# Attention stage: the next mask's fetch put one step ahead of its conversion, and the grid's ReLU and normalization put later in ScalarE's order

## The chip, the cores and the metric

The kernel runs on one core of one Trainium2 chip. The time is that of one execution on the device in microseconds (us), the median of several runs: three here, 2698.76 to 2705.61 us, median 2701.66 us. A core has five engines with an instruction stream each: TensorE (PE in the profile; PEld are its weight loads), VectorE (DVE), ScalarE (ACT), GpSimd (POOL) and SyncE (SP, which only issues transfers here). Each executes its own stream strictly in its order; a semaphore holds an instruction until what it needs is there, and all that stands behind it on the same engine waits with it.

## The reference, cut to what matters

Four layers follow one another on eight batches of 512 x 512 values. The change lies where the first two overlap.

```python
# layer 0, the "grid": finite differences, then a ReLU
df = -gradv_Af + gradvv_Bf * 0.5
x = jnp.maximum(f + df * dt[:, None, None], 0.0)
# layer 1, attention with 16 heads of 32
x = _ln(src) * (1.0 + scale) + shift
scores = einsum('bhqd,bhkd->bhqk', q / sqrt(32), k) + attention_bias
scores = where(src_mask, -inf, scores)
probs = softmax(scores)
...
x = x + (ctx @ Wo + bo)
```

After it come the rest of layer 1 and two layers more (gelu feed-forward by expert, a gated low-rank response). The mask is one byte per score, 512 x 512 for a batch, the same for all heads.

## The kernel before, in words

`attention_stage` works in *units*. A unit is one batch `b`, one group `c` of four heads and one quarter `r` of the query rows: 16 units make a batch, and I number them as *steps* t = 4c + r, 0 to 15. The order of the work is written out by hand in the loop at L1137: nearly every instruction is pinned to program order on its engine (`pin`), so a line's place in the loop is its place in the engine's stream.

In iteration i of the loop three units are under way. `scores` (L1003) has put four heads' scores into four PSUM banks `s0` to `s3` at the end of the iteration before. `softmax(now, u)` for u = 0 and 1 (L1015) takes two heads each: VectorE forms bias minus scores with its minimum (L1022, `bt<-s,bt`, `mn`), which frees the scores' bank, and ScalarE takes the exponential (L1027). `turned(old, u)` (L1033) transposes the probabilities of the unit before on TensorE into one of two PSUM buffers of the tag `tr`, and VectorE or ScalarE copies them out (`pt`, L1052 and L1054); TensorE cannot transpose into a buffer before its last copy is done. `values` (L1056) multiplies probabilities by v, in odd steps. `add_mask` (L994) lets GpSimd add the mask to the bias of the next unit, and `load_bias` (L982) has SP fetch the bias of three units on.

Between these stand two kinds of extra work:

- `fill(b, t)` (L927) yields a batch's projections and what prepares the next batch n = b + 1. In step 9, inside `k_block`, `x1_in(n, c)` (L601) transposes the next batch's normalized input four times (`xtr`) into the same two `tr` buffers; VectorE (L614) and ScalarE (L612) read them in turn. In steps 11 to 14 `x1_back` (L617) turns it back, and in steps 12 to 15 `load_mask(n, t - 12)` first issues the transfer of a quarter of the next batch's mask (`mask_in`, `mu`, 64 KB, on SP) and at once its conversion to bf16 times -1e30 on ScalarE (`mask_out`, `mk`, L593).
- `grid_step` (L854) runs layer 0 for the next batches in small operations on VectorE, listed in `GRID` (L830) by a phase j. Seen from a batch's own steps, phase 8 of the next batch lies at the end of step 0, phase 14 at the end of step 6, 15 and 16 at the end of steps 7 and 8. `x0` and `x1` (phases 8 and 14) finish two of four row slices; ScalarE then applies the ReLU (L804) and issues a transfer of one edge row into that slice (L806, `x<-xed`, 2 KB). `s1` (phase 15) takes the statistics of the slice on VectorE (L812), which need the ReLU and, for the second half, the edge row. `n0` and `n1` (phases 15 and 16) form a shift on VectorE (L819, `gsh`), and ScalarE normalizes two rows (L823).

`grid_gate(i)` (L741) is a one-column addition on GpSimd at the start of an iteration. It reads the last result of VectorE's grid work, so that GpSimd's additions (L998) start only after it. In iteration 7 of a batch the result that it reads is the slice that the ReLU has just been given.

The program gives each transfer of SP and ACT one of eight completion counters in turn, and an issue first waits for the previous transfer with its counter.

Of the kernel before, what the change touches and what calls it, by code (L numbers as in the profile page):

```python
# [15 lines left out]
AF = mybir.ActivationFunctionType  # L16
# [4 lines left out]
NB = 8  # L21
S = 512
D = 512
P = 128
R = 4
# [519 lines left out]
def attention_stage(  # L545
# [12 lines left out]
    nc = tc.nc  # L558
    with ExitStack() as ctx:
# [4 lines left out]
        pin = tc.keep_in_program_order  # L564
# [21 lines left out]
        def mask_in(b, r):  # L586
            mu = pp.tile([P, S], U8, name=f"mu_{b}_{r}", tag="mu", bufs=2)
            pin(nc.sync.dma_start(mu, a["mask"][b, 0].rearrange("(p r) k -> r p k", r=R)[r]))
            mask[b, r] = mu
# [3 lines left out]
            pin(nc.scalar.activation(m, mask[b, r], AF.Copy, scale=NEG))  # L593
            mask[b, r] = m

        def load_mask(b, r):
            mask_in(b, r)
            mask_out(b, r)


        def x1_in(b, c):  # L601
            tag, bufs = ("tr", 2) if b or c < 2 else (f"s{c}", 1)
# [87 lines left out]

        gs = {}
        L, M = slice(0, D - 1), slice(1, D)

        def gv(out, x, y, op):
# [72 lines left out]
        def grid_op(n, op):  # L769
            key, p = op[0], int(op[1])  # L770
            f = gs[n, "f"]
            rows = slice(2 * p, 2 * p + 2)
            e = xt[n][:, rows, :] if p < 2 else None
            if key == "q":
                t = gs[n, "q", p]
                gv(t, t, f[:, rows, :], ALU.mult)
            elif key in "egcab":
                o = 2 * p + dict(e=0, g=2).get(key, 1)
                t = gs[n, key, p]
                gv(t, t, f[:, o : o + 2, :], ALU.mult)  # L780
            elif key == "w":
                t = gs[n, "q", p]
                gv(t, gs[n, "q", p + 1], t, ALU.subtract)
            elif key in "CG":
                gv(e, e, gs.pop((n, key.lower(), p)), ALU.add)
            elif key == "+":
                gv(e[:, :, L], e[:, :, L], gs[n, "q", p][:, :, M], ALU.add)
            elif key == "-":
                gv(e[:, :, M], e[:, :, M], gs.pop((n, "q", p))[:, :, L], ALU.subtract)
            elif key == "A":  # L790
                gv(e[:, :, M], e[:, :, M], gs.pop((n, "a", p))[:, :, L], ALU.add)
            elif key == "B":
                gv(e[:, :, L], e[:, :, L], gs.pop((n, "b", p))[:, :, M], ALU.add)
            elif key == "x":
                ends = e[:, :, 0 : D : D - 1]
                gv(ends, ends, gs[n, "ghost"][:, rows, :], ALU.add)
                pin(
                    nc.vector.scalar_tensor_tensor(
                        e, e, grid["dth"][:, n : n + 1], f[:, 2 * p + 1 : 2 * p + 3, :],
                        ALU.mult, ALU.add,  # L800
                    )
                )
                gs["last"] = e[:, 0, 0:1]
                pin(nc.scalar.activation(e, e, AF.Relu))  # L804
                x, k = ((xt[n][0:1, 0, :], n), (xt[n][P - 1 : P, R - 1, :], NB + n))[p]
                pin(nc.scalar.dma_start(x, grid["xed"][k : k + 1, :]))  # L806
            elif key == "s":
                st = small.tile([P, 2, 6], F32, name=f"gst_{n}_{p}", tag="gst", bufs=2)
                mv = small.tile([P, 2, 2], F32, name=f"gmv_{n}_{p}", tag="gmv", bufs=2)
                rs = small.tile([P, 2], F32, name=f"grs_{n}_{p}", tag="grs", bufs=2)  # L810
                for r in range(2):
                    pin(nc.vector.bn_stats(st[:, r, :], e[:, r, :]))  # L812
                    pin(nc.vector.bn_aggr(mv[:, r, :], st[:, r, :]))
                gs[n, "st"] = mv, rs
            elif key == "n":
                mv, rs = gs[n, "st"]
                sh = small.tile([P, 2], F32, name=f"gsh_{n}_{p}", tag="gsh", bufs=2)
                pin(
                    nc.vector.scalar_tensor_tensor(sh, mv[:, :, 0], -1.0, rs, ALU.mult, ALU.mult)  # L819
                )  # L820
                for r in range(2):
                    pin(
                        nc.scalar.activation(  # L823
                            e[:, r, :], e[:, r, :], AF.Identity, bias=sh[:, r : r + 1],
                            scale=rs[:, r : r + 1],
                        )
                    )


        GRID = {  # L830
# [96 lines left out]
        def fill(b, t):  # L927

            n = b + 1
            jobs = []  # L930
            if b == 0:
                if t == 0:
                    homes = (("m", 1), ("tr", 2), ("tr", 2), ("ctx", 1))
                    for m in range(4):
                        jobs.append(v_block(0, m, *homes[m]))
                        jobs.append(grid_early(j) for j in (m + 3,))
                    jobs.append(grid_early(7) for _ in range(1))
                    jobs.append(mask_out(0, r) for r in (2, 3))
                elif t == 1:
                    jobs.append(add_bv() for _ in range(1))  # L940
                elif t in (2, 3, 4, 7):
                    jobs.append(x1_back(0, (2, 3, 4, 7).index(t)) for _ in range(1))
            if n == NB:
                if t == 0:
                    head["fill"] = halves(b)
                jobs.append(
                    next(head["fill"], None)
                    for _ in range({0: 2, 7: 2, 8: 2, 11: 2, 12: 2, 13: 0, 14: 2, 15: 0}.get(t, 1))
                )
            elif t in (0, 4, 8):  # L950
                jobs.append(q_block(b, t // 4 + 1))
            elif t in (1, 5, 9):
                turn = (lambda c: x1_in(n, c)) if t == 9 else None
                jobs.append(k_block(b, t // 4 + 1, turn=turn))
            elif t in (2, 3, 6, 7):
                if b:
                    jobs.append(o_block(b - 1, (2, 3, 6, 7).index(t)))
            elif t == 11:
                jobs.append(q_block(n, 0))
            elif t == 13:  # L960
                jobs.append(k_block(n, 0))
            else:
                jobs.append(v_block(n, (10, 12, 14, 15).index(t)))
            if n < NB:
                if t in (11, 12, 13, 14):
                    jobs.append(x1_back(n, t - 11) for _ in range(1))
                if t >= 12:
                    jobs.append(load_mask(n, t - 12) for _ in range(1))
            elif t == 8:
                jobs.append(head_stats() for _ in range(1))  # L970
            elif t in (10, 11):
                jobs.append(head_norm(r) for r in (2 * t - 20, 2 * t - 19))
            elif t in (13, 15):
                jobs.append(head_turn(c) for c in (t - 13, t - 12))
            for j in jobs:
                yield from j
# [135 lines left out]
        n = len(units)  # L1112
# [24 lines left out]
        for i in range(n + 2):  # L1137
            now = units[i] if i < n else None
            old = units[i - 1] if 1 <= i <= n else None
            two = units[i - 2] if i >= 2 else None  # L1140
            jobs = fill(now[0], 4 * now[1] + now[2]) if now else iter(())
            grid_gate(i)
            if i + 1 < n:
                add_mask(*units[i + 1])
            grid_step(i - 1, grid_pow)
            pair = two and two[2] % 2 == 1
            if pair:
                values(two[0], two[1], two[2] // 2)
            for u in range(2):
                if old:  # L1150
                    turned(*old, u)
                if now:
                    softmax(*now, u)
                next(jobs, None)
            if old and old[2] == R - 1:
                inverse(*old[:2])
            drain(jobs)
            split = pair and two[2] == R - 1
            if split:
                grid_step(i, lambda n, j: grid_sums(n, j, late=False))  # L1160
                divide(two[0], two[1])
            if i + 3 < n:
                load_bias(*units[i + 3])
            if now and now[0] and now[1:] == ((2, 1) if now[0] < NB - 1 else (3, 3)):
                nc.sync.dma_start(x1d[now[0] - 1], xt[now[0] - 1])
            if now and now[0] == NB - 1:
                head_load(4 * now[1] + now[2])
            grid_step(i, lambda n, j: grid_sums(n, j, early=not split))
            grid_step(i, grid_loads)
            if i + 1 < n:  # L1170
                scores(*units[i + 1])
# [893 lines left out]
```

## Time and profile before

| what | us |
|---|---|
| median of three runs | 2701.66 |
| the profiled execution | 2701.51 |
| its span, first to last instruction | 2699.7 |
| TensorE busy in it | 2649.8 |
| VectorE, GpSimd, ScalarE busy | 1930.8, 1480.9, 960.9 |
| attention: first scores to last | 70.8 to 1077 |
| feed-forward and the rest | 1106 to 2699 |

The profile comes from one execution. Its page has busy times, the chain of work that ended last, and groups of instructions with the idle time before them and what ended it. The chain of waits lists, per engine, who waited for whom: total us, times, longest. The timeline lists instructions by start and duration, with the idle time before one in square brackets and who ended it. Step lengths below are read off the timeline as the distance between the first scores matmuls (`s<-kt,qt`) of two units that follow each other. From 1106 us to the end TensorE works without a gap in stretches of 48.35 us, which the change doesn't touch.

### The profile page before, as it was taken

The page shows a single profiled execution, that of the slowest core. Times are in us where ns is not written, and L with a number is a line of the kernel's source. Part 1 is how long each engine was busy: PE and PEld are TensorE (multiplying, and loading weights), DVE is VectorE, ACT ScalarE, POOL GpSimd, SP SyncE. Part 2 cuts the span into 40 slices and gives each one's busy share as a digit, 9 for nine tenths or more (in the row PEclk, how much of TensorE's full clock was granted, in tenths as well). Part 3 has the DMA queues.
Part 4 walks back from the last instruction along what each step waited for, and adds up shares of the span by engine and source line. Part 5 has one row for each costly group of instructions (what it writes and reads, how often), then busy time and mean ns, then how long its engine had stood idle before and what let it go on. Part 6 is the DMA issues. An engine that isn't in the chain of part 4 may idle for free.

```text
span 2699.7 us, 39350 instructions
## 1 busy us (share of the span) xinstructions
PE 2649.8 (98%) x14182; PEld 1959.2 (73%) x14182; DVE 1930.8 (72%) x3538; ACT 960.9 (36%) x1997; POOL 1480.9 (55%) x1090
## 2 busy tenths in 40 slices
PE   7999999999999999999999999999999999999998
PEld 4455555555555555788888888888888888888887
DVE  7888898989898756576666656656555766666665
ACT  2566666666666666212212211210111211211221
POOL 3455565655555655366566465555555555555543
PEclk9999999999999999999999999999999999999999
DMA  8765757666676554644453543455335346345421
GB/s 308 253 217 194 247 193 242 212 215 231 230 240 211 167 170 157 194 144 117 138 156 98 162 146 100 148 156 154 120 116 184 127 150 194 124 145 198 121 100 42
DMA packets 241760, 460.31 MB, mean 171 GB/s; under 512 B 33848, under 2 KB 77440, under 8 KB 232478
## 3 DMA queue, kind: packets, MB, share of 16 engines
q1 hardware_dynamic: 237754, 447.04, 49.2%
q0 software_dynamic: 3360, 10.68, 3.0%
q8 instruction: 113, 1.85, 0.3%
q14 instruction: 81, 0.66, 0.1%
q10 hardware_dynamic: 452, 0.07, 0.0%
HBM read 398.43 MB, written 55.09 MB: 168 GB/s over the span
## 4 chain that ended last, share of the span: by engine, by line
PE 90%; DVE 4%; DMA 3%; ACT 1%; SPq 1%; issue 1%; POOL 0%; ACTq 0%; DVEq 0%; POOLq 0%
PE u L1208 29%; PE y L1208 28%; PE tr L570 8%; PE s L567 5%; PE o L567 4%; PE ctx L567 4%; PE pq L567 4%; PE pv L567 3%; PE pk L567 3%; DMA mu<-in_mask 2%; DVE bt L1022 1%; PE l L251 1%; DMA rd<-rt 1%; DVE x L697 1%; DVE pt L1052 1%
## 5 line engine op out<-in xcount | busy, mean ns | idle before, releaser
L998 POOL TENSOR_TENSOR bt<-bt,mk 128x1024 f32<-128x1024 f32 x256 | 543.7, 2148 | 72.6 <-DMA bt<-in_bias 67.2
L1208 PE MATMUL y<-wo,act 128*128 128x256 f32 x2560 | 566.3, 380 | 0.0
L1208 PEld LDWEIGHTS y<-wo,act 128*128 128x128 f32 x2560 | 484.5, 190 | 71.6 <-issue 6.7
L1027 ACT ACTIVATE bt<-bt,mn 128x512 f32<-128x512 f32 x512 | 365.7, 716 | 87.7 <-DVE mn L1022 86.4
L570 PEld LDWEIGHTS tr<-ident,bt 128*128 128x128 f32 x2048 | 229.4, 142 | 159.9 <-issue 97.5
L1022 DVE CUSTOM_DVE_ANT_0 bt<-s,bt 128x512 f32<-128x512 f32 x512 | 330.8, 684 | 2.2 <-PE s L567 2.0
L1208 PE MATMUL u<-bt,wi 128*128 128x256 f32 x1440 | 330.5, 379 | 0.0
L1214 DVE TENSOR_TENSOR act<-u,u 128x512 f32<-128x512 f32 x256 | 173.2, 684 | 200.6 <-PE u L1208 132.5
L1208 PEld LDWEIGHTS u<-bt,wi 128*128 128x128 f32 x1440 | 273.5, 190 | 37.2
L570 PE MATMUL tr<-ident,bt 128*128 128x128 f32 x2048 | 278.2, 278 | 15.1 <-ACT pt L1054 12.9
L1208 PE MATMUL u<-tb,ws 128*128 128x256 f32 x1024 | 242.2, 379 | 0.0
L1054 ACT COPY pt<-tr 128x512 f32<-128x512 f32 x306 | 172.6, 581 | 179.0 <-PE tr L570 176.3
L1208 PE MATMUL y<-t,s 128*128 128x256 f32 x1024 | 227.8, 380 | 0.0
L1217 POOL TENSOR_TENSOR t<-wo,t 128x512 f32<-128x512 f32 x64 | 107.3, 1699 | 203.1 <-PE y L1208 203.1
L1052 DVE COPY pt<-tr 128x512 f32<-128x512 f32 x206 | 141.9, 689 | 106.2 <-PE tr L570 100.2
L1208 PEld LDWEIGHTS u<-tb,ws 128*128 128x128 f32 x1024 | 194.3, 190 | 26.6 <-DVE tb L1214 0.2
L1208 PEld LDWEIGHTS y<-t,s 128*128 128x128 f32 x1024 | 194.0, 190 | 26.1
L1572 ACT ACTIVATE act<-act,b 128x512 f32<-128x512 f32 x128 | 82.9, 712 | 292.8 <-DVE act L1214 292.8
L1572 ACT ACTIVATE act<-act,bi 128x512 f32<-128x512 f32 x128 | 83.8, 712 | 282.6 <-DVE act L1214 282.6
L567 PE MATMUL s<-kt,qt 32*128 32x512 f32 x1024 | 175.9, 640 | 2.0 <-DVE mn L1022 1.0
L1591 ACT COPY u<-u 128x512 f32<-128x512 f32 x64 | 36.4, 568 | 393.3 <-PE u L1208 278.2
L1214 DVE TENSOR_TENSOR x<-y,x 128x512 f32<-128x512 f32 (+1 forms) x97 | 64.7, 680 | 154.0 <-PE y L1208 103.7
(323 smaller groups left out, 4144.5 us busy)
## 6 DMA issues: line engine op xcount, KB each, us to landing
bt<-in_bias SPq DMA_DIRECT2D x256, 512.0 KB
wo<-in_W SPq DMA_DIRECT2D x32, 1024.0 KB
wi<-in_Wi SPq DMA_DIRECT2D x32, 1024.0 KB
wo<-in_Wo_e SPq DMA_DIRECT2D x32, 1024.0 KB
wi<-in_W SPq DMA_DIRECT2D x28, 1024.0 KB
td<-tt SPq DMA_DIRECT2D x22, 1024.0 KB
bt<-td SPq DMA_DIRECT2D x176, 128.0 KB
gq<-coef_q SPq DMA_DIRECT2D x21, 512.0 KB
```

What stands on the lines that cost most here:

```text
L567: pin(nc.tensor.matmul(out, lhsT=lhsT, rhs=rhs, start=start, stop=stop))
L570: pin(nc.tensor.transpose(out, src, ident))
L998: nc.gpsimd.tensor_tensor(bt, bt, mask[b, r][:, None, :].to_broadcast([P, 2, S]), ALU.add)
L1022: nc.vector.tensor_tensor_reduce(bt[:, i, :], ss[h], bt[:, i, :], -1.0, 3.0e38, ALU.add, ALU.min, mn)
L1027: nc.scalar.activation(bt[:, i, :], bt[:, i, :], AF.Exp, bias=mn, scale=-1.0, accum_out=sums[b, c][:, h, r : r + 1],)
L1052: pin(nc.vector.tensor_copy(pt[:, :, r % 2, :], tr))
L1054: pin(nc.scalar.copy(pt[:, :, r % 2, :], tr))
L1208: pin(nc.tensor.matmul(out, lhsT=lhsT, rhs=rhs, start=start, stop=stop))
L1214: pin(nc.vector.tensor_tensor(out, x, y, op))
L1217: pin(nc.gpsimd.tensor_tensor(out, x, y, op))
L1572: nc.scalar.activation(acts[g][:, k, :], acts[g][:, k, :], func, bias=bi[:, j : j + 1])
L1591: pin(nc.scalar.copy(u1, p[0]))
```

## The change

Three things move; no instruction is added or taken away, and the order on TensorE, VectorE and GpSimd stays what it was.

- `load_mask` is split. The transfer of quarter r of the next mask is issued in step 11 + r, and its conversion stays in step 12 + r. On SP each of the 28 transfers moves up by one step, past that step's two bias transfers and what lies between.
- The ReLU with its edge row transfer goes from the end of steps 0 and 6 into the next step, behind the exponentials of the first two heads (u = 0). On ScalarE it moves past one or two copies `pt` and two exponentials.
- The normalization goes in the same way from the end of steps 7 and 8 into steps 8 and 9.

With the ReLU behind it in program order, the gate of iteration 7 now waits for VectorE's result and not for the ReLU, and the ReLU waits for the gate to have read it. The transfers' counters shift too: SP's second `gq` load behind the `gf` loads in step 7 shared a counter with the edge row and now shares one with a `gf` load.

```diff
-        def load_mask(b, r):
-            mask_in(b, r)
-            mask_out(b, r)
...
-        gs = {}
+        gs, later = {}, []
...
                 gs["last"] = e[:, 0, 0:1]
-                pin(nc.scalar.activation(e, e, AF.Relu))
-                x, k = ((xt[n][0:1, 0, :], n), (xt[n][P - 1 : P, R - 1, :], NB + n))[p]
-                pin(nc.scalar.dma_start(x, grid["xed"][k : k + 1, :]))
+
+                def relu():
+                    pin(nc.scalar.activation(e, e, AF.Relu))
+                    x, k = ((xt[n][0:1, 0, :], n), (xt[n][P - 1 : P, R - 1, :], NB + n))[p]
+                    pin(nc.scalar.dma_start(x, grid["xed"][k : k + 1, :]))
+
+                later.append(relu)
...
-                for r in range(2):
-                    pin(
-                        nc.scalar.activation(
-                            e[:, r, :], e[:, r, :], AF.Identity, bias=sh[:, r : r + 1],
-                            scale=rs[:, r : r + 1],
+
+                def norm():
+                    for r in range(2):
+                        pin(
+                            nc.scalar.activation(
+                                e[:, r, :], e[:, r, :], AF.Identity, bias=sh[:, r : r + 1],
+                                scale=rs[:, r : r + 1],
+                            )
                         )
-                    )
+
+                later.append(norm)
...
                 if t >= 12:
-                    jobs.append(load_mask(n, t - 12) for _ in range(1))
+                    jobs.append(mask_out(n, t - 12) for _ in range(1))
+                if 11 <= t < 15:
+                    jobs.append(mask_in(n, t - 11) for _ in range(1))
...
                 if now:
                     softmax(*now, u)
+                while u == 0 and later:
+                    later.pop(0)()
                 next(jobs, None)
```

## The prediction

> **What bounds the kernel now.** First the page: who owns the chain that ended last.
>
> ```profile
> span 2699.7 us, 39350 instructions
> ...
> PE 2649.8 (98%) x14182; PEld 1959.2 (73%) x14182; DVE 1930.8 (72%) x3538; ACT 960.9 (36%) x1997; POOL 1480.9 (55%) x1090
> ...
> PE 90%; DVE 4%; DMA 3%; ACT 1%; SPq 1%; issue 1%; POOL 0%; ACTq 0%; DVEq 0%; POOLq 0%
> ```
>
> TensorE is the bound, so a change elsewhere counts only where it makes TensorE wait. Next the chain of waits:
>
> ```profile
> ACT mk L593 <- DMA mu<-in_mask: 56.7, 14, 6.3
> ...
> POOL gate L746 <- ACT x L804: 26.4, 7, 3.8
> ...
> PE tr L570 <- ACT pt L1054: 12.9, 14, 2.1
> ```
>
> ScalarE stands 56.7 us in front of the mask's conversion, and TensorE 12.9 us in front of ScalarE's copies. The timeline of batch 3 joins the two (steps 13 and 14):
>
> ```profile
> 567.28 1.14 PE L567 MATMUL s<-kt,qt 32*128 32x512 f32 x8
> ...
> 573.18 0.63 ACT L593 ACTIVATE mk<-mu 128x512 bf16<-128x512 uint8 x1 [5.09 <-DMA mu<-in_mask]
> ...
> 574.34 0.66 PE L570 MATMUL tr<-ident,bt 128*128 128x128 f32 x4 [0.87 <-ACT pt L1054]
> ...
> 577.11 1.14 PE L567 MATMUL s<-kt,qt 32*128 32x512 f32 x8
> ...
> 581.00 0.63 ACT L593 ACTIVATE mk<-mu 128x512 bf16<-128x512 uint8 x1 [2.84 <-DMA mu<-in_mask]
> ...
> 582.16 0.66 PE L570 MATMUL tr<-ident,bt 128*128 128x128 f32 x4 [0.73 <-ACT pt L1054]
> ...
> 584.93 1.14 PE L567 MATMUL s<-kt,qt 32*128 32x512 f32 x8
> ```
>
> Mask late, copy late, transpose late: the steps take 9.83 and 7.82 us. With no wait on TensorE they take 8.73 (step 11 of batch 6, same work) and 6.87 (step 14 of batches 1 and 6). Last, steps 8 and 9, where the normalization goes:
>
> ```profile
> 524.28 8.43 POOL L998 TENSOR_TENSOR bt<-bt,mk 128x1024 f32<-128x1024 f32 x4
> ...
> 528.02 0.52 DVE L819 SCALAR_TENSOR_TENSOR gsh<-gmv,grs 128x2 f32<-128x2 f32 x1
> ...
> 534.63 0.15 DVE L819 SCALAR_TENSOR_TENSOR gsh<-gmv,grs 128x2 f32<-128x2 f32 x1
> ...
> 534.82 1.52 ACT L823 ACTIVATE x<-x,gsh,grs 128x512 f32<-128x512 f32 x2 [0.30 <-DVE gsh L819]
> ...
> 542.69 0.76 ACT L612 ACTIVATE x<-xtr,ada 128x512 f32<-128x512 f32 x1
> ...
> 543.50 0.42 PEld L570 LDWEIGHTS xtr<-ident,x 128*128 128x128 f32 x4 [0.38 <-ACT x L612]
> ```
>
> The normalization at 534.82 lies in a hole of ScalarE; at 543.50 TensorE waits for ScalarE.
>
> **The mask.** With the transfer a step earlier (7.9 us: batch 3's 16 steps lie between 467.5 and 593.2) the longest wait of 6.3 us is covered. The 0.63 us conversions stay where they are, in ScalarE's idle time. On SP the transfer moves ahead of two bias loads, and in step 12 ahead of the row sums' transfers; its 64 KB stand against 512 KB each, its issue takes 0.43 us, and as many leave the step behind: nothing. Were the cover gone, the waits would come back, up to the 15.4 below. Its buffer (two of them) is free one conversion earlier, so SP waits for ScalarE no longer than before the next bias load, which itself waited for GpSimd's gate until 579.39. The lengths of steps 12 to 14 over 6.87, 8.73 and 6.87 are 2.5, 3.9, 2.5, 2.1, 1.4, 1.3 and 1.8 us for batches 0 to 6: 15.4 us. Bounds: 11.1 (TensorE's own waits in these steps) and 19.9 (step 11's excess too, which is VectorE's). I take 15.4. In batch 1 part of it is the clock:
>
> ```profile
> 318.90:322.30 3.40, 1.40 (x7) 0.63 (x5) 2.66 (x9) 1.08 (x3) 2.78 (x2) 1.00 0.63 154
> 322.30:325.70 3.40, 3.33 (x7) 1.92 (x8) 0.00 (x0) 3.33 (x10) 0.00 (x0) 0.50 0.93 336
> ```
>
> 3.4 us with TensorE busy for 1.40 are followed by 3.4 us at half the granted clock (0.50): 1.9 of batch 1's 3.9 us. [...]
>
> **The normalization in step 9.** `n1` now stands between exponentials and copy. In batch 3 ScalarE's first two exponentials end at 540.17; 1.52 us of normalization end at 541.70; copy (0.57), two exponentials (1.43) then bring L612 to 543.49 instead of 542.69, since 0.16 and 0.26 us of waits before them are used up. The last `xtr` follows L612: 0.80 us, seven batches, +5.6. Bounds: 0 and 7 x 1.52 = 10.6. Queued behind it are the copy, whose buffer the second `xtr` wants, and kt, which the scores want only at the end of step 11. `n0` in step 8 costs nothing: its cover is the stretch until 537.83, when ScalarE next waits for TensorE; without it, up to 10.6 as well.
>
> **The gate.** It now waits for VectorE (522.97), not for the ReLU (524.07): GpSimd's four additions of 2.09 us start 1.1 us earlier. `gsh` at 528.02 took 0.52 instead of 0.15 us because it got through only when an addition ended (528.52). Shifted, the additions end at 527.41 and 529.50: `gsh` ends 0.98 us later. When the statistics were 0.53 and 0.47 us late (batches 1, 4), TensorE lost 0.12 and 0.03 us in step 9, so 0.42 is slack: 0.56 for batches 1 to 6 less what two had already, 0.4 for batch 0: +3.6. Bounds 0 and 7 x 0.98 = 6.9.
>
> **The ReLU and its edge row.** ReLU 1.06 us and issue 0.22: in steps 1 and 7 they put off a copy whose buffer is next wanted over 4 us later, and exponentials that are transposed a step later; 0, and at most 14 x 1.28 = 18 were that cover gone. Gain from earlier copies: TensorE waited 0.06 us in step 7; -0.3 with batch 0. The row is issued at about 526.6 instead of 524.09. Ahead of it are the `gf` loads, drained at 529.1 (DMA share 0.95 before, 0.37 after); it should land by 530.2, when the late `gsh` has the second statistics begin (530.25): 0. SP's second `gq` load, which waited for the row through their common counter, comes up to 1 us sooner; it is wanted a step later: 0.
>
> **Step 11.** In batches 1 to 5 it is 0.6 to 1.2 us long (4.2 together), since VectorE meets an addition that started late behind a bias transfer (0.65 us at 549.16). A TensorE 1.3 us later meets it less: -2.6, between 0 and -4.2.
>
> **Sum**, on the profiled execution's 2701.5 us, which stands 0.15 below the median: -15.4 + 5.6 + 3.6 - 0.3 - 2.6 = -9.1, so 2692.5 us.
>
> **The rivals.**
> *Later conversions free* (steps 8 and 9 give their loss back in step 11 and VectorE's slack): the mask alone, 2701.5 - 15.4 = 2686.1. For it: ScalarE is 36% busy. Against: the wait at 543.50 has no slack.
> *Gain eaten*: both prices at their upper ends, 2701.5 - 15.4 + 10.6 + 6.9 = 2703.6. Against: the holes of 0.16 and 0.26 us.
> *Slower: the edge row lands late.* Were it issued after SP's next load (528.75, 2.1 us later than I work out), it would queue behind `gq` and bias, 1 MB at some 300 GB/s = 3.5 us, and VectorE would wait in step 8 until about 533.9 instead of 530.25: in batches 1 to 6 6 x 3.65 = 22 more than the sum, 2692.5 + 22 = 2714. For it: the row issued at 271.41 held VectorE until 277.12, as if it stood behind all loads issued before. [...]
> *The mask's transfer still late*, behind its counter's previous transfer: that one is over 3 us old in program order, so no chance of its own.
>
> **How the numbers follow.** 0.3% is 8.1 us, about what a measurement here can tell from no change. The sum 0.50 (own range 2689 to 2697, so 0.33 faster, 0.17 same); free 0.27, faster; eaten 0.15, same; row late 0.08, slower. Faster 0.60, same 0.32, slower 0.08. Range 2684 (mask and something of step 11) to 2704 (gain eaten): it leaves the late row and part of the eaten gain out.
>
> **What would show it.** No wait of `mk` on `mu`; steps 13 and 14 at 8.73 and 6.87; no half clock in batch 1; `gsh` of step 8 ending about 1 us later and step 9 of batches 1 to 6 longer; `xtr` waiting about 1 us for L612. Wrong: step 9 unchanged (free), or VectorE's statistics waiting for the edge row.

## The result and the profile after

The changed kernel takes 2690.48 us (median of nine runs, 2688.70 to 2691.75); the kernel before, run as often, takes 2698.77 us (2694.92 to 2705.61). The ratio is 0.9965, with a 95% interval of 0.9955 to 0.9975: 6.7 to 12.1 us faster, 9.4 in the middle, where the prediction had 9.1; the two medians lie 8.3 us apart. The line numbers of the changed kernel differ a little: the ReLU is L802 and its edge row L804, the normalization L825, the addition of the mask L1004, the gate L742, the copies L1058 and L1060, the two readers of `xtr` L610 (VectorE) and L608 (ScalarE, L612 before).

The page of the changed kernel, the lines that answer to those of before:

```profile
span 2688.7 us, 39347 instructions
...
PE 2648.5 (99%) x14182; PEld 1960.3 (73%) x14182; DVE 1937.9 (72%) x3538; ACT 961.1 (36%) x1997; POOL 1478.8 (55%) x1090
...
PE 92%; DVE 4%; DMA 2%; ACT 1%; issue 1%; POOL 0%; SPq 0%; ACTq 0%; DVEq 0%; POOLq 0%
```

TensorE is still the bound. It is as busy as before (2648.5 against 2649.8 us) and the span is 11.0 us shorter, so what went is time in which it waited or ran slowly. The chain of waits of the changed kernel:

```profile
PEld xtr L570 <- ACT x L825: 3.5, 7, 0.5
...
ACT mk L593 <- DMA mu<-in_mask: 2.9, 1, 2.9
...
PEld xtr L570 <- ACT x L608: 2.6, 7, 0.4
...
PE tr L570 <- ACT pt L1060: 1.8, 2, 1.5
...
DVE gst L812 <- DMA x<-xed: 0.8, 3, 0.4
```

The mask's 14 waits of 56.7 us have become one, at 74 us in front of batch 0's own mask, and TensorE's 14 waits for the copies, 12.9 us, have become two. One line is new in kind: weight loads of `xtr` now wait seven times for the normalization itself (L825). Their seven waits for ScalarE's copy L608 are as long as they were for L612 before (2.6 us). The grid's statistics waited for the edge row before the change too, 1.3 us in three waits; that this is less now doesn't mean that the row is sooner, for the statistics are later themselves. The timeline of batch 3, steps 13 and 14:

```profile
559.83 1.14 PE L567 MATMUL s<-kt,qt 32*128 32x512 f32 x8
...
560.54 0.63 ACT L593 ACTIVATE mk<-mu 128x512 bf16<-128x512 uint8 x1
...
568.57 1.14 PE L567 MATMUL s<-kt,qt 32*128 32x512 f32 x8
...
569.38 0.61 ACT L593 ACTIVATE mk<-mu 128x512 bf16<-128x512 uint8 x1
...
575.44 1.14 PE L567 MATMUL s<-kt,qt 32*128 32x512 f32 x8
```

The conversions wait for nothing, and the steps take 8.74 and 6.87 us where they took 9.83 and 7.82. Both lengths return in every one of the seven batches. Steps 8 and 9 of the same batch went the other way:

```profile
518.52 0.22 ACTq L804 DMA_DIRECT2D x<-xed  x1
...
519.07 1.14 PE L567 MATMUL s<-kt,qt 32*128 32x512 f32 x8
...
519.79 1.57 DVE L819 SCALAR_TENSOR_TENSOR gsh<-gmv,grs 128x2 f32<-128x2 f32 x1
...
521.28 0.68 DVE L812 BATCH_NORM_STATS2 gst<-x 128x6 f32<-128x512 f32 x1
...
522.57 0.69 DVE L812 BATCH_NORM_STATS2 gst<-x 128x6 f32<-128x512 f32 x1 [0.40 <-DMA x<-xed]
...
525.48 2.25 PE L567 MATMUL s<-kt,qt 32*128 32x512 f32 x8
...
526.60 0.29 PEld L567 LDWEIGHTS s<-kt,qt 32*128 32x128 f32 x2 [0.32 <-DVE mn L1028]
...
533.10 1.50 ACT L825 ACTIVATE x<-x,gsh,grs 128x512 f32<-128x512 f32 x2
...
534.51 0.56 ACT L1060 COPY pt<-tr 128x512 f32<-128x512 f32 x1
...
537.81 1.14 PE L567 MATMUL s<-kt,qt 32*128 32x512 f32 x8
```

The first shift `gsh` takes 1.57 us where it took 0.52, the second statistics wait for the row, and the scores of step 9, which need the banks that VectorE empties next, are spread over 2.25 us. Then the normalization at 533.10 stands before a copy of ScalarE. Step 9 takes 12.33 us where it took 10.38.

Summed over the seven batches, from step lengths of the profiles (excess is what lies over the stall-free length):

| us | before | after | difference |
|---|---|---|---|
| excess of steps 12 to 14 (over 6.87, 8.74, 6.87) | 15.4 | 0.05 | -15.4 |
| step 9 over 10.38 | 0.2 | 10.6 | +10.4 |
| step 11 over 8.74 | 4.4 | 0.2 | -4.2 |
| steps 0 to 8 of batch 0 | 85.0 | 82.3 | -2.7 |

### The profile page after: what moved, and what is told of

Read it like the earlier page. It is cut to its first block, busy times and chain, and to the rows that moved or that the text cites. A ratio compares the mean times of both kernels' runs of the same rounds, so it can differ in the third digit from the quotient of the medians.

```text
span 2688.7 us, 39347 instructions
## 1 busy us (share of the span) xinstructions
PE 2648.5 (99%) x14182; PEld 1960.3 (73%) x14182; DVE 1937.9 (72%) x3538; ACT 961.1 (36%) x1997; POOL 1478.8 (55%) x1090
## 4 chain that ended last, share of the span: by engine, by line
PE 92%; DVE 4%; DMA 2%; ACT 1%; issue 1%; POOL 0%; SPq 0%; ACTq 0%; DVEq 0%; POOLq 0%
PE u L1216 29%; PE y L1216 29%; PE tr L570 8%; PE s L567 6%; PE ctx L567 4%; PE o L567 4%; PE pq L567 4%; PE pv L567 4%; PE pk L567 3%; DVE bt L1028 1%; PE l L251 1%; ACT bt L1033 1%; DVE x L693 1%; PE xb L570 1%; DMA a<-in_A 0%
## 5 line engine op out<-in xcount | busy, mean ns | idle before, releaser
L1004 POOL TENSOR_TENSOR bt<-bt,mk 128x1024 f32<-128x1024 f32 x256 | 541.6, 2140 | 71.7 <-DMA bt<-in_bias 45.3
L1060 ACT COPY pt<-tr 128x512 f32<-128x512 f32 x306 | 173.0, 582 | 251.1 <-PE tr L570 246.6
L1058 DVE COPY pt<-tr 128x512 f32<-128x512 f32 x206 | 142.0, 689 | 105.4 <-PE tr L570 100.3
```

The costliest lines, as they stand in the source:

```text
L1004: nc.gpsimd.tensor_tensor(bt, bt, mask[b, r][:, None, :].to_broadcast([P, 2, S]), ALU.add)
L1058: pin(nc.vector.tensor_copy(pt[:, :, r % 2, :], tr))
L1060: pin(nc.scalar.copy(pt[:, :, r % 2, :], tr))
```

## The experiments

The change falls apart into three: the mask's transfer, the ReLU (with gate and edge row), the normalization. Four kernels take them one by one.

### The mask alone

ReLU and normalization are called where they stand, as before; the mask's part stays.

```diff
-                later.append(relu)
+                relu()
...
-                later.append(norm)
+                norm()
```

> Only the mask's transfer a step earlier; ReLU and normalization at their old places. Theory (the parts add up step by step): steps 12 to 14 stand at 6.87, 8.74, 6.87 us in all seven batches (-15.4 against the kernel before), step 9 at 10.4 as before, and step 11's excess of 4.2 us together is back (9.3 to 9.9 in batches 1 to 5), since TensorE is no longer late from step 9: about -15.4 us, ratio 0.9943. Rival A (step 11's excess belonged to the mask's transfers on SP): step 11 at 8.74 too, -19.6 us, ratio 0.9927. Rival B (the mask's waits went because the later ReLU and normalization let ScalarE go ahead): waits in front of the conversion remain, -8 us or less.

Measured: 2683.5 us against 2697.59 (0.995, interval 0.9934 to 0.9967). Steps 12 to 14 have no excess (0.04 us over all), step 9 is 10.38. Its chain of waits:

```profile
POOL gate L742 <- ACT x L802: 26.4, 7, 3.8
...
ACT mk L593 <- DMA mu<-in_mask: 2.7, 1, 2.7
...
PE tr L570 <- ACT pt L1060: 1.8, 2, 1.5
```

So the mask's waits go without any help from the later ReLU and normalization: rival B is out. Step 11 had 1.56 us of excess, between what the theory (4.2) and rival A (0.2) asked for. The same kernel was run once more:

> The kernel with the mask's part alone, once more, beside the next one. Steps 12 to 14 without excess, step 11 with 0 to 3 us over all batches, step 9 at 10.38: 2683 to 2685 us, ratio 0.994 to 0.996, below the changed kernel's 0.9965.

Measured: 2683.3 us, 0.9944 (0.9931 to 0.9957), and step 11 now had 4.47 us. Rival A is out as well: the excess of step 11 is there with the mask's transfers moved.

### Later ReLU and normalization alone

```diff
-                    jobs.append(mask_out(n, t - 12) for _ in range(1))
-                if 11 <= t < 15:
-                    jobs.append(mask_in(n, t - 11) for _ in range(1))
+                    jobs.append(load_mask(n, t - 12) for _ in range(1))
```

> Only ReLU and normalization later; the mask's transfer stays in front of its conversion. Theory: step 9 is 11.9 to 12.3 us in batches 1 to 6 (10.4 us over before together), step 11 at 8.74 (-4.2), steps 12 to 14 with their old excess of 15.4 us: +6.2 us, ratio 1.0023. Rival A: step 11 keeps 9.3 to 9.9, +10.4 us, ratio 1.0039. Rival B: steps 12 to 14 lose part of their excess, no slower than before.

Measured: 2707.02 us against 2697.59, 1.0037 (1.0023 to 1.0051): slower by 6 to 14 us. Its steps are those of the theory: step 9 10.45 us over 10.38 together, step 11 0.41, steps 12 to 14 16.2. The chain of waits shows the mask's waits untouched:

```profile
ACT mk L593 <- DMA mu<-in_mask: 55.7, 14, 6.0
...
PE tr L570 <- ACT pt L1062: 13.2, 14, 2.1
```

The changed kernel is thus a gain of some 14 us and a loss of 7 to 9 (2690.48 against the 2683.5 of the mask alone, 2707.02 against 2697.59), in steps that don't touch each other, and the loss is all in the part that moved ReLU and normalization. The two measured apart add up to 4.7 us of gain where the whole has 8.3 to 9.4; their intervals are some 4 us wide to each side, so the times alone don't tell whether the parts affect each other.

### Normalization later, ReLU as before; and of the normalization the first half alone

```diff
-                later.append(relu)
+                relu()
```

> Mask earlier and normalization later, ReLU at its old place. Theory: first shift of step 8 takes 0.5 us, no wait for the edge row, step 9 is 0.8 us over 10.4 in each of seven batches (5.9 us together): -15.4 + 5.9 = -9.5, less 0 to 4.2 from step 11: -9.5 to -13.7 us. Rival (the VectorE's lateness behind ReLU and gate is all of step 9's loss): step 9 at 10.4, -15.4 us.

Measured: 2685.05 us, 0.9954 (0.9937 to 0.9971). Step 9 is 11.22 or 11.23 us in all seven batches, 5.9 us together; step 11 has 1.0 us. The timeline of batch 3:

```profile
519.74 0.52 DVE L819 SCALAR_TENSOR_TENSOR gsh<-gmv,grs 128x2 f32<-128x2 f32 x1
...
521.00 0.66 DVE L812 BATCH_NORM_STATS2 gst<-x 128x6 f32<-128x512 f32 x1
...
525.43 1.14 PE L567 MATMUL s<-kt,qt 32*128 32x512 f32 x8
...
531.95 1.50 ACT L825 ACTIVATE x<-x,gsh,grs 128x512 f32<-128x512 f32 x2
...
533.50 0.14 PEld L570 LDWEIGHTS xtr<-ident,x 128*128 128x128 f32 x1 [0.50 <-ACT x L825]
...
536.06 0.42 PEld L570 LDWEIGHTS xtr<-ident,x 128*128 128x128 f32 x4 [0.37 <-ACT x L608]
...
536.65 1.14 PE L567 MATMUL s<-kt,qt 32*128 32x512 f32 x8
```

With the ReLU back, the shift takes 0.52 us, no statistics wait, and the scores of step 9 are again in one piece of 1.14 us. What is left is 0.84 us at the transposes behind the normalization, and two paths lead there. On ScalarE the normalization, a copy and two exponentials follow each other without a pause, and L608 starts 9.82 us into step 9 instead of 8.98; the last `xtr` needs the buffer that it reads. But TensorE's wait for L608 is 0.37 us, no longer than before (0.38), because TensorE is late itself by then: the fourth transpose reads a row that is only now being normalized (the wait at 533.50), the fifth needs the buffer of the copy behind, and the products between the transposes start 0.85 us late (9.04 us into the step instead of 8.19). ScalarE's path ends last and is enough for the 0.84 us; without it, TensorE's own would still cost some 0.5 (an estimate: the last `xtr` would follow its predecessor at once).

The next kernel leaves only the first half of the normalization (n0, step 8) later; the ReLU stays as in the diff above.

```diff
-                later.append(norm)
+                later.append(norm) if p == 0 else norm()
```

> Mask earlier, and of the normalization only the first half (in step 8) later; ReLU and second half (step 9) at their old places. Theory (the second half's 0.84 us per batch is all that the later normalization costs): step 8 at 6.41 and step 9 at 10.38 us, time as with the mask alone (2683.5). Rival (the first half costs too, since two copies stand behind it): step 8 or 9 longer by 0.2 us or more in each batch.

Measured: 2683.36 us, 0.9955 (0.9939 to 0.9972), with steps 8 and 9 at 6.41 and 10.38 in batches 1 to 6. The first half costs nothing and brings nothing; the second half is the 0.84 us.

### ReLU later, normalization as before

```diff
-                later.append(norm)
+                norm()
```

> Mask earlier and ReLU later, normalization at its old place. Theory: the first shift of step 8 takes 1.55 us and the second statistics wait some 0.4 us for the edge row, so that step 9 is 0.5 to 1.1 us over 10.4 in batches 1 to 6, 4.5 us together; nothing of the 0.84 us per batch that the normalization holds up the last transposes of the next input. Against before -15.4 + 4.5 = -10.9, less what step 11 gives back (0 to 4.2): -10.9 to -15.1 us. Rival (the normalization is all of step 9's loss): step 9 at 10.4, -15.4 us.

Measured: 2686.25 us, 0.9959 (0.9945 to 0.9973). The sum was as expected, the place was not: step 9 is 10.38 in most batches, and step 8 is 7.15 instead of 6.41 in batches 1 to 6 (4.4 us together). The timeline says why:

```profile
519.67 1.56 DVE L819 SCALAR_TENSOR_TENSOR gsh<-gmv,grs 128x2 f32<-128x2 f32 x1
...
521.27 1.52 ACT L825 ACTIVATE x<-x,gsh,grs 128x512 f32<-128x512 f32 x2 [0.60 <-DVE gsh L819]
...
522.70 1.05 ACT L1060 COPY pt<-tr 128x512 f32<-128x512 f32 x2
...
523.40 1.06 PE L570 MATMUL tr<-ident,bt 128*128 128x128 f32 x8 [0.56 <-POOL bt L1004]
```

With the normalization at its old place ScalarE waits for the late shift, its two copies behind the normalization come late, and TensorE starts the transposes 0.7 us later, with a wait of 0.56 us in front of them, already in step 8. (The profile puts that wait down to the addition that ended 0.05 us after the first copy. In the changed kernel the same transposes start 3.7 us into step 8 although that addition ends 4.4 us into it, so it isn't the addition that they need.) So the two moves are not independent: put later, the first half of the normalization lets the copies pass, and the late shift is felt a step further on.

### What of the ReLU's move costs: the earlier additions or the late row

The gate no longer waits for the ReLU, so GpSimd's additions start 1.1 us earlier; and the edge row is issued 2.6 us later within step 7. The next kernel keeps the first and takes most of the second away: the ReLU stands right behind the gate.

```diff
-        gs, later = {}, []
+        gs, later, soon = {}, [], []
...
-                later.append(relu)
+                soon.append(relu)
...
             grid_gate(i)
+            while soon:
+                soon.pop(0)()
```

> As the changed kernel (mask earlier, normalization later), but the ReLU with its edge row right behind the gate, before the exponentials of the first two heads. The gate still doesn't wait for the ReLU; the row is issued some 2 us sooner. Theory (two causes behind the ReLU: additions earlier cost 0.58 us per batch, the late edge row the rest): first shift of step 8 takes 1.55 us, second statistics wait for no row, step 9 is 11.8 us in each of batches 1 to 6 (0.58 over the 11.22 of the kernel with only the normalization later); 3.5 us over that kernel, some 2688.5. Rival (all of it is the row): step 9 at 11.22.

Measured: 2689.31 us, 0.997 (0.9959 to 0.9981). No statistics wait for the row. Step 9 is 11.47 to 11.50 us, 0.26 over the kernel with the normalization alone, and step 7 is 9.12, 0.28 longer, because the ReLU now waits for the gate to have read its data and copies stand behind it. Together 0.54 us per batch in place of the 0.58 expected. The additions alone therefore cost about 0.54 us, and the rival (all of it is the row) is out. Batch 6 of the changed kernel, where nothing waits for the row, shows it directly: its step 9 takes 11.81 us, 0.59 over 11.22.

Next the additions were held back with more gates. First nine gates on top of that kernel:

```diff
-                pin(nc.gpsimd.tensor_tensor(g, t, t, ALU.add))
+                for _ in range(9 if i % 16 == 7 else 1):
+                    pin(nc.gpsimd.tensor_tensor(g, t, t, ALU.add))
```

> The same, and the gate's one-column addition nine times over in iteration 7 of each batch, which holds GpSimd's additions back by about 1.1 us, to where they were before. Theory (the shift waits because an addition is under way when VectorE wants it): shift of step 8 at 0.4 to 0.7 us, step 9 back at 11.2 to 11.3 us in batches 1 to 6, time as with only the normalization later (2685). Rival (the order of ReLU and gate itself costs, by another path): step 9 stays at 11.8 us, some 2688.5.

Measured: 2705.06 us, 1.0034 (1.0021 to 1.0046), neither theory. The run tested something else: each further gate took 0.27 us, twice what had been counted, and the ReLU had to wait for all nine. Its timeline of batch 3, ScalarE and then TensorE:

```profile
526.03 1.06 ACT L803 ACTIVATE x<-x 128x1024 f32<-128x1024 f32 x1 [5.46 <-POOL gate L743]
```

```profile
528.02 0.66 PE L570 MATMUL tr<-ident,bt 128*128 128x128 f32 x4 [2.25 <-ACT pt L1061]
```

TensorE waited 2.25 us in step 7 of each of batches 1 to 6 for the copy behind the ReLU. It shows only that the wait of the ReLU for the gate, new with the change, is a real one. The next kernel is the changed one itself with five gates, which end before its later ReLU comes.

```diff
-                pin(nc.gpsimd.tensor_tensor(g, t, t, ALU.add))
+                for _ in range(5 if i % 16 == 7 else 1):
+                    pin(nc.gpsimd.tensor_tensor(g, t, t, ALU.add))
```

> The changed kernel as it is, with the gate's one-column addition five times over in iteration 7 of each batch. Nine of them took 2.4 us and held the ReLU behind them; five take 1.3 us instead of 0.19 and end before the ReLU comes. GpSimd's additions are then 1.1 us later, where they were before. Theory (the first shift of step 8 is slow because an addition is under way): it takes 0.4 to 0.6 us instead of 1.55 and the first statistics start 1.2 us into step 8 instead of 2.2; what is left is the edge row, which lands 2.5 to 3.5 us into step 8: step 9 between 11.3 and 12.3 us, differing by batch, time 2687 to 2690. Rival (the shift waits for something else in the changed order): shift at 1.5 us, step 9 as in the changed kernel, 2690.5.

Measured: 2689.71 us, 0.9969 (0.996 to 0.9978). Its timeline of batch 3, where step 8 begins at 521.78:

```profile
517.57 1.29 POOL L743 TENSOR_TENSOR gate<-x 128x1 f32<-128x1 f32 x5 [2.68 <-DVE x L795]
...
518.81 8.42 POOL L1005 TENSOR_TENSOR bt<-bt,mk 128x1024 f32<-128x1024 f32 x4
...
521.78 1.14 PE L567 MATMUL s<-kt,qt 32*128 32x512 f32 x8
...
522.50 0.56 DVE L820 SCALAR_TENSOR_TENSOR gsh<-gmv,grs 128x2 f32<-128x2 f32 x1
...
522.98 0.68 DVE L813 BATCH_NORM_STATS2 gst<-x 128x6 f32<-128x512 f32 x1
...
525.07 0.69 DVE L813 BATCH_NORM_STATS2 gst<-x 128x6 f32<-128x512 f32 x1 [1.19 <-DMA x<-xed]
```

With the additions 1.1 us later the shift takes 0.56 us instead of 1.57 and the first statistics start 1.20 us into step 8 instead of 2.21: the shift had waited for an addition under way, and the rival is out. In the changed kernel the shift began at 519.79 and ended at 521.36, just after the third of the four additions (521.34).

But step 9 is not much shorter (9.3 us over 10.38 in batches 1 to 6, against 9.7), because now the row is seen by itself: it lets the second statistics start 3.06 to 3.57 us into step 8 in batches 1 to 5, while they would be ready at 2.0. In batch 6 nothing waits for it, and step 9 is 11.22 us. That batch is the one in which no `gf` loads are issued in step 7. The DMA share in the changed kernel, batch 3 and then batch 6, before the row's issue (columns: stretch; its length, then busy time and instructions of PE, PEld, DVE, ACT, POOL; granted clock; DMA share; GB/s):

```profile
515.00:518.50 3.50, 3.50 (x15) 1.97 (x14) 3.08 (x9) 2.98 (x6) 3.50 (x3) 1.00 0.75 246
...
887.60:891.00 3.40, 3.40 (x15) 1.94 (x14) 2.98 (x9) 2.85 (x6) 3.40 (x2) 1.00 0.53 154
```

So the `gf` loads hold the row up, but they are not all of its way: in the kernel with five gates its signal comes 2.6 us after its issue in batch 6, without them, and 3.6 to 4.1 us after it in batches 1 to 5. Additions alone cost 3.2 us over batches 1 to 6, the row alone 4.2, both 4.7: they end in the same wait of VectorE, and the later one sets it. In all 18 cases (batches 1 to 6 of these three kernels) step 9's excess over 11.22 us is, within 0.02 us, how late the second statistics start after 2.41 us into step 8, and nothing where they start sooner.

### Step 11, and an attempt at a faster kernel

The kernel before was profiled a second time:

> The kernel before, once more, for its profile: how much of step 11's excess (4.2 us in batches 1 to 5 of the first profile, 1.35 us in the kernel with only the mask changed) belongs to the kernel and how much to the execution. If it belongs to the kernel before (the mask's transfers behind the bias loads): again 0.5 to 1.2 us in each of batches 1 to 5. If it differs from execution to execution: batches with none and a sum anywhere between 1 and 4 us.

This execution took 2693.5 us. Step 11 had 0.45, 0.00, 0.40, 1.42 and 0.88 us of excess in batches 1 to 5, and steps 12 to 14 had 10.8 us instead of 15.4:

```profile
ACT mk L593 <- DMA mu<-in_mask: 53.9, 14, 5.2
...
PE tr L570 <- ACT pt L1054: 9.6, 15, 1.9
```

Both terms differ from execution to execution. Over the profiles in which step 9 stayed at 10.38 us and steps 7 and 8 at their old lengths, step 11 had 4.4, 3.4, 1.6, 4.5 and 3.0 us of excess; over those with step 9 longer by more than a microsecond in most batches 0.2, 0.4, 0.7, 0.2 and 1.1. The two in between, with only the normalization or only the ReLU later, had 1.0 and 1.6.

Steps 3 and 7 are 0.5 us longer than the others like them. In step 7 an addition of the grid, phase 14's first, takes 2.0 us (1.97 at 519.48 in batch 3 of the kernel before, with an addition of GpSimd under way until 520.36; 1.21 at 567.99, with GpSimd idle); the attempt moves it to the step before.

```diff
-        13: "a1 | A1 b1", 14: "B1 x1", 15: "n0 s1", 16: "n1",
+        13: "a1 | A1 b1 B1", 14: "x1", 15: "n0 s1", 16: "n1",
```

> An attempt at a faster version: the mask's part alone, and one addition of the grid (the last but one of phase 14) put from the end of step 6 to the end of step 5. In step 6 it takes 2.0 instead of 1.2 us since an addition of GpSimd is under way, and VectorE's copies behind it are late in step 7 (8.84 us). If that is why step 7 is long: step 7 at about 8.3 us in batches 1 to 6, 3 us faster than the mask alone (2681). Rival (the collision only moves to step 5, whose end already holds two or three such additions): step 6 longer by 0.5 to 1.2 us instead, no faster than the mask alone.

Measured: 2703.22 us, 1.0016 (1.0008 to 1.0025). The moved addition did take 1.2 us, but the gate of step 6 waited for it, GpSimd's additions started later, and in batches 1 to 6 step 7 became 1.3 us or more longer and step 8 0.6 us or more. Neither expectation named that. Step 11 had 6.1 us here with nothing added in step 9; why is open. The kernel with the mask alone (2683.5 and 2683.3 us) stays the fastest, level with the one that also has the first half of the normalization later (2683.36): 7 us ahead of the changed one by the medians, 4 to 6 by the ratios to the kernel before.

## Why the prediction was right

**The bound and the reading.** Mask late, copy late, transpose late was the chain; with the transfer a step earlier all three waits go, in seven batches of seven. The mask's move by itself shows it.

**The mask, -15.4.** -15.4 between the two profiles. It is the size in that execution of the kernel before; the second one has 10.8, the kernel that leaves the mask alone 16.2. By the medians, the mask alone is worth 14.1 and 15.3 us in two comparisons. The forecast was made against 2701.5 us, and the kernel before has a median of 2698.8, so 2692.5 came out 2 us above the 2690.5 measured. That the difference of 9.1 meets the measured 9.4 so closely is luck in part: the changed kernel's profiled execution takes 11.0 us less than the one the forecast was read from and only 3.0 less than the second execution of the kernel before, and of the terms below some miss by 1 to 3 us, not all the same way.

**The normalization in step 9, +5.6.** 0.84 us in each of seven batches, 5.9; n0 at nothing, as named. The path that was named sets it, L608 starting 0.84 us later behind the normalization. The sign that was named for it, `xtr` waiting about 1 us for that copy, didn't come: the wait stayed at 0.37 us, since the prediction left out that the transposes also need the normalized row itself and the copy behind, which make TensorE as late on its own.

**The gate, +3.6.** The mechanism was right: the shift ended 1.06 us later where 0.98 was worked out, VectorE had 0.42 to 0.46 us of slack where 0.42 was read off, and the additions alone cost 0.54 to 0.59 us in each of batches 1 to 6 where 0.56 was put. Batch 0, put at 0.4, lost nothing in step 9 beyond the 0.84.

**The edge row, 0.** This step failed, though it moved little: VectorE's statistics waiting for the row had been named as a sign of being wrong, and they do. The row was to land by 530.2, 2.9 us into step 8; in batches 1 to 5 the statistics got it 3.06 to 3.50 us into it in the changed kernel, and up to 3.57 in the one with five gates. It added 1.2 to 1.5 us to the 3.2 to 3.5 of the additions, and by itself it would have cost 4.2. The rival that priced a late row had the direction but not the size (3.65 us per batch; 0.5 us at most came). The landing at 530.2 was the author's estimate from the drain of the `gf` loads at 529.1, and no run shows the 1.1 us between the two: in the changed kernel the row, issued at 518.52, let the statistics go at 522.57, 4.05 us later, and in the kernel with five gates it takes 2.6 us even in batch 6, without `gf` loads. What else it waits for on its way, the runs don't show.

**The earlier copies, -0.3.** Step 7 fell from 8.84 to 8.80 us in batches 1 to 6 and from 10.52 to 10.48 in batch 0: -0.3.

**Step 11, -2.6.** -4.2 between the two profiles; over the profiles listed above the mean falls from 3.4 to 0.5 us. That a longer step 9 gives this back is what the pattern says; the attempt with 6.1 us shows that the account of step 11 is not complete.

**What the sum left out.** Batch 0 gave 2.7 us in its first steps, with a half clock (0.50 granted) at 93.6 us (94.0 in the second profile) that both profiles of the kernel before show and the changed one doesn't. Three experiments that contain the mask's change show it too, so it isn't shown to belong to the change. In batch 7, where nothing was moved, step 5 was 1.6 us longer and step 14 1.6 us shorter than before, each with a half clock in one of the two profiles (at 1069.83 us before, at 992.66 in the changed kernel).

**The rivals.** "Later conversions free" is out by step 9, "gain eaten" by sizes: the two losses were 10.6 and 6.9 at their bounds and came to 5.9 and, over what step 9 took before, 4.5 with the row's part in it, and step 11 gave back. What decided against the free case, that the wait at 543.50 has no slack, held.

## What to carry to other kernels

The conversion that followed its own transfer in the same step held ScalarE, with all that stood behind it, for 56.7 us in 14 waits, 6.3 us at most; fetching one step ahead cost nothing and was worth 14 us. That an engine is mostly idle (ScalarE is 36% busy) doesn't make it free to move an instruction later in its order. Ask what needs its result (here transposes that read the normalized row), what stands behind it (a copy that frees a PSUM buffer), and what had been waiting for it as a gate: taking that wait away started GpSimd's additions 1.1 us sooner, and one of them then held up VectorE's shift (1.57 us instead of 0.52). A change made of several moves is best costed step by step and then measured move by move: here one of three carried all the gain.

## What the runs showed of the hardware

**The clock after short waits.** TensorE fell to half clock (0.50 granted) for 3.41 us after some waits of about 2 us and not after others. The kernel with nine gates has the same 2.25 us wait in six batches, and only one is followed by half clock (windows of its batch 5 and then 6, columns as above):

```profile
776.20:779.60 3.40, 1.66 (x7) 0.70 (x5) 2.97 (x9) 1.18 (x2) 2.86 (x8) 1.00 0.85 292
779.60:783.00 3.40, 2.88 (x16) 1.39 (x16) 0.67 (x3) 3.40 (x9) 3.40 (x3) 1.00 0.83 256
...
902.50:905.90 3.40, 1.39 (x7) 0.63 (x5) 2.91 (x9) 1.44 (x2) 2.93 (x8) 1.00 0.49 154
905.90:909.30 3.40, 3.15 (x7) 1.91 (x8) 0.00 (x0) 3.40 (x10) 3.40 (x3) 0.51 0.19 45
```

TensorE was busy for 1.66 us of 3.4 in the first case and 1.39 in the second, and where batch 1 of the kernel before fell to half clock it was 1.40. The kernel with only the later ReLU and normalization had it again, in step 14 of batch 2, where a wait of 2.06 us left TensorE 1.34 us of 3.4 busy: 4.0 us of excess instead of some 2. In the profile of the kernel before the half-clock stretches at 93.63, 141.41 and 322.32 us begin 47.78 and 180.91 us apart, close to 14 and 53 times their own 3.41 us. Busy time as the profile counts it doesn't tell the cases apart by itself: the half clock at 141.41 follows 3.41 us in which TensorE counts as busy for 3.32. What decides after which wait the clock falls, the runs don't show.

**A small operation's price.** VectorE's shift of 128x2 values takes 0.15 us with GpSimd idle (at 527.61 in the changed kernel), 1.57 us in step 8 of the changed kernel, and 2.05 us at most (batch 0 of the kernel with only ReLU and normalization later), when a 2.1 us addition of GpSimd is under way. The shift is the same each time; what differs is when it starts.

**A chain of gates.** A one-column addition of GpSimd takes 0.19 us by itself; five that follow each other took 1.29 us in the kernel with five gates, 0.27 us for each further one.
